# A two-image sparse attention kernel: new order ranks, a smaller ranking, products in pieces, and scatters and fetches of the first image that wait for the landing two places ahead

## The chip, the cores and the metric

The kernel runs on one core of a Trainium2 chip. Its time is the device time of one execution in microseconds (us), taken as the median over several runs. The profile is one execution of the same program, recorded by the hardware profiler; the times of instructions come from there. Engines are named as in the profile: PE is TensorE, PEld its weight load, DVE is VectorE, ACT is ScalarE, POOL is GpSimd, SP is SyncE, which only issues transfers here.

## The reference, cut to what matters

Two layers, each on images of 256 channels and 64 x 64 positions (N = 4096), two images. The first attends with sparsemax, the second with an unnormalised ReLU of a sum:

```python
# layer 0 (e: 64-channel conv 3x3 + batch norm + PReLU of x)
sim = einsum('bdn,bdm->bnm', e, e)
p   = sparsemax(sim, axis=2)          # threshold tau by the sorted row, max(sim - tau, 0)
x   = einsum('bcn,bnm->bcm', x, p) + x
# layer 1
g   = einsum('oc,bcn->bno', g_w, x) + g_b              # 128 channels
a   = w_t . theta(x);  bsc = w_p . phi(x)              # one number per position
f   = relu(a[:, :, None] + bsc[:, None, :] + wf_b)     # N x N
y   = matmul(f / N, g)
z   = batch_norm(wz @ y) + x
```

## The kernel before, in words

`sparse_path` computes everything; a dense path behind it stands for rows that the sparse one can't hold and is not run with this input.

**Layer 0.** After the convolution, `survey` (tiles sv) finds for each position whether its sparsemax row is the trivial one (only itself). `listed` gathers the few other rows into three blocks of 128. `rows` computes their similarities (PE, tile rw, L476; copy to z, L774; running maxima on DVE, L777), bisects the threshold and applies it. `attend` multiplies the kept columns: on POOL a product of x with a mask (L831, one per two 512-column blocks and channel half, with a small tick copy L826 ahead), on PE the product av (L836), on DVE the addition into x (L843). One matrix multiplication of the program is two MATMUL instructions in the trace.

**Layer 1.** f is a ReLU of a sum of two numbers, so y needs no N x N matrix: if positions are sorted by bsc, then the y of a position is made of two prefix sums over the sorted g. `project` (image 0, g, L873) and `project_in` (image 1, g, L899) compute g with the two extra columns (tile ga). The class `Ranked` then does, for its R row tiles of 128 positions (image 0: R = 32, all; image 1: R = 24, and the last 8 tiles are done densely: f on ACT L1512, py on PE L1520, `rest`):

- `keys` (L1000 on): sortable keys, made distinct from each other's neighbours by their low bits. `spread` turns them to rows on PE, writes them to memory (row_k to rd_k, L932) and reads them back to all partitions as kb (L944), both issued from SP.
- `above` for each row tile t: a pass over the columns of kb from tile t on that counts how many keys are larger, on ACT (Sign with accumulation, L1050) or DVE (is_gt with accumulation, L1054). Two slots or four of the junk ring take the results. `below` sums the same results over partitions on PE (L1065, L1076) for the later tiles; `below_out` (L1087) and `below_turned` (bt, L1093) bring these sums back to a column.
- `ties` (L1101): a DVE operation over the 128x128 block of the own tile, that adds equal keys further down by the triangular matrix `low`.
- `place` (L1115 to L1120) adds it all to a rank; `scatter` (L1125/L1126) writes the g row of each position to its rank in the memory table sg, an indirect DMA that POOL issues, one per row tile, with a memset ahead.
- `load` (L1141 to L1144) reads the sorted table into tab, in parts of 16 tiles (TH = 16); `products` (L1152/L1153) multiplies the g part by its key column, one operation per part; `sums` (L1160) adds up along the tiles, one dependent addition per tile; `before` (po, L1164) and `raised` (L1167) add what the partitions ahead hold; `stored` (L1173) writes the table tb.
- `segments` (oh, L1187/1188), `places` (pk, L1196) and `counts` (L1205 to L1208) find for each position its place k in the table; `fetch` (L1213) is an indirect DMA from POOL that brings the 128 rows of one tile of positions to a slot of r (16 slots; image by image 32 fetches).
- `taken` (L1226 on) combines a fetched row, turns it on PE (yr, L1233, yT, L1238 or L1240), and `finish` multiplies by wz (pz, L960), adds into x (L964) and stores to out (L967).

**What sets the order.** The class `Plan` writes the instruction order of every engine ahead of time: a list scheduler over tasks with a cost per engine, a latency (`lat`), and a rank; where several tasks can begin at about the same moment the lowest rank goes first. The ranks are 21 constants in L281 (RW1 for the rows of image 1, A1 for its attention, R0 and R1 for the beginnings of the rankings, K0 and K1 for their passes, CH0 and CH1 for the chains of load, products, sums, store and fetch, P1 and P2 for the projection, SP1 for spreading a, PY and PF for the dense part, BE for below, and so on). Where a task may go to DVE or ACT, the planner chooses too. At run time each engine executes its own list in order, and waits at an instruction until what it needs is there. SP's list holds the issue of the ordinary transfers, POOL's the mask products, scatters and fetches.

Of the kernel before, what the change touches and what calls it, by code (L numbers as in the profile page):

```python
# [8 lines left out]
F32 = mybir.dt.float32  # L9
BF16 = mybir.dt.bfloat16  # L10
# [4 lines left out]
ALU = mybir.AluOpType  # L15
# [4 lines left out]
P = 128  # L20
# [19 lines left out]
CS = 2 * CI + 1  # L40
TH = 16
# [149 lines left out]
def sparse_path(ctx: ExitStack, tc, a, out, rows_i):  # L191
    nc = tc.nc
# [787 lines left out]
    class Ranked:  # L980
# [55 lines left out]
        def above(self, t, on_act, d):  # L1036

            slot = d["slot"] = self.slot(self.used)
            self.used += 1
            kb, cnt, n = self.kb, self.cnt, self.R * P
            d["on_act"] = on_act
            c = ds(t * P, n - t * P)
            if on_act:
                nc.scalar.activation(  # L1050
                    slot[:, c], kb[:, c], AF.Sign, scale=STEEP, bias=self.bound[:, 1, t : t + 1], accum_out=cnt[:, t, 3:4],
                )
            else:
                nc.vector.tensor_scalar(  # L1054
                    slot[:, c], kb[:, c], self.key[:, t : t + 1], None, ALU.is_gt, ALU.add, accum_out=cnt[:, t, 1:2],
                )
            if on_act:
                self.on_act.append(t)
# [36 lines left out]
                    start=True, stop=True,  # L1095
                )

        def ties(self, t):

            junk = small.tile([P, P], BF16, name=f"tied_{self.b}_{t}", tag="tied", bufs=1)  # L1100
            nc.vector.scalar_tensor_tensor(  # L1101
                junk, self.kb[:, ts(t, P)], self.key[:, t : t + 1], low,
                ALU.is_equal, ALU.mult, accum_out=self.cnt[:, t, 2:3],
            )

        def place(self, t0, bt):

            b, R = self.b, self.R
            for t in range(t0, t0 + 4):
                known = t * P - sum(u in self.on_act for u in range(t)) * (P // 2)
                known += (R - t) * P // 2 if t in self.on_act else 0
                nc.vector.memset(self.cnt[:, t, 0:1], float(known))  # L1115
            cnt = self.cnt[:, ds(t0, 4)]
            rk = small.tile([P, 4], F32, name=f"rk_{b}_{t0}", tag="rk", bufs=2)
            nc.vector.tensor_reduce(rk, cnt[:, :, 0:3], AX.X, ALU.add)  # L1118
            nc.vector.tensor_tensor(rk, rk, bt, ALU.add)
            nc.vector.scalar_tensor_tensor(self.rank[:, ds(t0, 4)], cnt[:, :, 3], 0.5, rk, ALU.mult, ALU.add)  # L1120

        def scatter(self, t):
            b = self.b
            gap = small.tile([1, 1], F32, name=f"gap_{b}_{t}", tag="gap")
            nc.gpsimd.memset(gap, 0.0)  # L1125
            rows = nc.gpsimd.indirect_dma_start(  # L1126
                out=self.sg,
                out_offset=bass.IndirectOffsetOnAxis(ap=self.rank[:, t : t + 1], axis=0),
                in_=self.ga[:, t, 0 : CI + 2],
                in_offset=None,  # L1130
            )
# [11 lines left out]
            nc.vector.memset(self.nxt, -3.0e38)  # L1143
            nc.sync.dma_start(out=self.nxt[0 : P - 1], in_=sv[1:P, 0, CI + 1 : CI + 2])  # L1144

        def products(self, h):
            b, R, tab = self.b, self.R, self.tab[h]
# [3 lines left out]
            t0, n = self.parts[h]  # L1151
            nc.vector.tensor_copy(self.kr[:, ds(t0, n)], tab[:, :, CI + 1])  # L1152
            nc.vector.tensor_mul(  # L1153
                tab[:, :, CI + 1 : CS], tab[:, :, 0:CI], tab[:, :, CI : CI + 1].to_broadcast([P, n, CI])
            )

        def sums(self, t0, t1):
            at = lambda t: self.tab[t // TH][:, t % TH]
# [51 lines left out]
        def fetch(self, t):  # L1210
            if t == 0:
                self.r = self.at("r", [P, TH, CS], F32)
            nc.gpsimd.indirect_dma_start(  # L1213
                out=self.r[:, t % TH],
                out_offset=None,
                in_=self.tb,
                in_offset=bass.IndirectOffsetOnAxis(ap=self.k[:, t : t + 1], axis=0),
            )
# [31 lines left out]
            finish(b, ds(i * CB, CB), scaled, "A" if rest is None else "D", rank, after, h)  # L1250

        def fetch_task(self, t, rank, after):
            self.fetched[t] = plan.task({"G": 1.27}, lambda: self.fetch(t), rank, after, lat=4.14)

        def begin(self, rank, after, ranked, chained, then, room):

# [3 lines left out]
            plan.task({"G": 0.2}, self.first, rank, [k], lat=2.3, take=hz, free=[hz])  # L1260
            sp = spread(f"k{self.b}", lambda: self.key, lambda: self.kb, 0, self.R, rank, [k])
            n = self.R * P
            self.places_done, self.ranked, places = [], [], []
            self.used = 0
            hb = ring_sim.hold()
            below, waiting, places = [], [], {}
            for t in range(self.R):
                r, m, d, q = ranked + t / 100.0, n - t * P, {}, t // 4
                hj, last = self.ring.hold(), t == self.R - 1
                u = plan.task(  # L1270
                    {"D": 0.25 + 0.00107 * m, "A": 0.66 + 0.00083 * m}, lambda e, t=t, d=d: self.above(t, e == "A", d), r,
                    [sp, *room], take=hj, free=[hj] if last else [],
                )
                self.ranked.append(u)
                tied = plan.task({"D": 0.36}, lambda t=t: self.ties(t), r + 0.02, [sp, *room])
                places.setdefault(q, []).extend([u, tied])
# [27 lines left out]

        def chain(self):
# [2 lines left out]
            ld = plan.task({"S": 0.1}, self.load, rk, self.places_done, lat=8.45)  # L1308
            t = ld
            for h in range(H):  # L1310
                t = plan.task({"D": 0.3 + 0.1375 * self.parts[h][1]}, lambda h=h: self.products(h), rk, [t])
# [60 lines left out]
    def constants():  # L1372
# [7 lines left out]
        for t, n, by_partition in ((iota, P, False), (lane, 1, True)):  # L1380
# [3 lines left out]
        nc.gpsimd.affine_select(  # L1384
            out=low, in_=onesq, pattern=[[-1, P]], compare_op=ALU.is_gt, fill=0.0, base=0, channel_multiplier=1
        )
        for k in range(8):
            nc.vector.memset(invk[:, k : k + 1], 1.0 / (k + 1))

# [116 lines left out]
    f = []  # L1506
# [445 lines left out]
```

## Time and profile before

| | |
|---|---|
| median of 14 runs | 710.24 us (703.04 to 713.14) |
| the profiled execution | 709.79 us, its span 708.1 us |
| mean granted TensorE clock | 0.904 |
| PE / DVE / ACT / POOL busy | 590.0 (83%) / 527.2 (74%) / 322.1 (45%) / 221.2 (31%) us |
| first rw of image 1 / first pass of ranking 0 | 373.95 / 392.0 us |
| first scatter / first load of image 0's table | 437.9 / 489.06 us |
| kb of image 1 issued / first use | 506.05 / 513.79 us |
| image 0's table raised / first fetch | 577.1 / 588.31 us |
| last fetch issued / end of span | 684.13 / 708.1 us |

The times in the last five rows are from the start of the span. A busy share is an average over stages: a stage is read from the time window in which it runs, and from the chain, which goes back from the last instruction to whatever released each step. "DMA to landing" is the time from the issue of a transfer to its completion.

### The profile page before, as it was taken

To read this page: it belongs to the slowest core of one execution; us is meant where nothing else is said; L and a number is where in the kernel's file an instruction comes from. 1 tells how busy PE (TensorE), PEld (TensorE's weight loads), DVE (VectorE), ACT (ScalarE), POOL (GpSimd) and SP (SyncE) were. 2 spreads that over 40 slices of the span, in tenths; PEclk is the share of its full clock that TensorE was granted. 3 is DMA by queue.
4 is the path that set the end of the run, shared out by engine and by line. 5 is a ranking of instruction groups with operands and counts; after the bars stand their busy time and mean duration, and the time that the engine had idled before them with its cause. 6 is when DMAs were issued, how large, how long until landed. Compare 5 with 4: busy or idle time off the path is not lost.

```text
span 708.1 us, 8398 instructions
## 1 busy us (share of the span) xinstructions
PE 590.0 (83%) x2835; PEld 282.1 (40%) x2835; DVE 527.2 (74%) x1074; ACT 322.1 (45%) x484; POOL 221.2 (31%) x290
## 2 busy tenths in 40 slices
PE   5998999999779799999987787999399994376762
PEld 4664444444332233343543223358244541254320
DVE  6985777877878978788758999833599852897761
ACT  0123576576439556467108985400398870000000
POOL 0117930000030130202030323684000776636750
PEclk9999999999879899999999798889699996667995
DMA  8621001101120000000023000014720166356861
GB/s 347 226 60 31 1 1 31 31 1 31 31 81 7 0 1 0 1 1 0 2 80 139 20 1 11 27 50 120 227 93 16 38 263 186 89 222 206 271 215 65
DMA packets 34268, 57.07 MB, mean 81 GB/s; under 512 B 12942, under 2 KB 21000, under 8 KB 33192
## 3 DMA queue, kind: packets, MB, share of 16 engines
q1 hardware_dynamic: 28440, 42.72, 18.1%
q0 software_dynamic: 5344, 13.14, 6.6%
q10 hardware_dynamic: 432, 0.59, 0.3%
q8 instruction: 24, 0.39, 0.2%
q14 instruction: 28, 0.23, 0.1%
HBM read 32.67 MB, written 21.66 MB: 77 GB/s over the span
## 4 chain that ended last, share of the span: by engine, by line
PE 54%; DVE 31%; DMA 6%; issue 5%; ACT 2%; POOL 0%; SPq 0%; DVEq 0%; ACTq 0%; POOLq 0%
PE sv L476 15%; PE av L836 10%; PE cv_in L363 6%; PE cv_out L363 6%; PE pz L960 4%; DVE junk L1054 4%; DVE mq L777 4%; DVE tied L1101 3%; DVE tab L1160 3%; DVE x L964 2%; PE g L873 2%; DVE tab L1167 2%; DVE xbs L524 2%; PE sv L508 2%; PE py L1520 2%
## 5 line engine op out<-in xcount | busy, mean ns | idle before, releaser
L528 ACT ACTIVATE sv<-sv,nthr 128x1024 f32<-128x1024 f32 (+1 forms) x133 | 131.2, 986 | 99.4 <-PE sv L508 47.9
L524 DVE TENSOR_TENSOR xbs<-sv,xbs 128x1024 f32<-128x1024 f32 (+1 forms) x120 | 130.7, 1089 | 37.4 <-PE sv L476 30.4
L476 PE MATMUL sv<-e 64*128 64x512 f32 x512 | 136.4, 643 | 5.8 <-ACT sv L528 4.4
L836 PE MATMUL av<-z,xbs 128*128 128x512 f32 x192 | 108.8, 690 | 4.9 <-DVE z L799 2.8
L1126 POOL DMA_INDIRECT sg<-ga,rank x56 | 55.6, 993 | 72.6 <-DVE rk L1118 51.6
L1213 POOL DMA_INDIRECT r<-tb,k x64 | 64.3, 1005 | 38.2 <-issue 14.3
L1050 ACT ACTIVATE junk<-kb,bound 128x2816 bf16<-128x2816 f32 (+26 forms) x39 | 69.9, 1799 | 10.8 <-PE below L1076 7.8
L476 PEld LDWEIGHTS sv<-e 64*128 64x128 f32 x512 | 45.7, 195 | 72.1 <-issue 42.7
L1520 PE MATMUL py<-f,ga 128*128 128x512 f32 x128 | 64.2, 642 | 0.0
L836 PEld LDWEIGHTS av<-z,xbs 128*128 128x128 f32 x192 | 36.6, 213 | 62.0 <-issue 49.0
L363 PE MATMUL cv_out<-v,wu 128*64 128x256 f32 (+1 forms) x384 | 49.2, 395 | 7.7 <-DVE v L325 7.7
L446 POOL TENSOR_TENSOR sq<-es 128x512 f32<-128x512 f32 x8 | 9.6, 1198 | 133.6 <-ACT es L437 111.2
L1238 ACT ACTIVATE yT<-yr 128x512 f32<-128x512 f32 x8 | 4.8, 597 | 95.8 <-PE yr L1233 89.0
L1233 PE MATMUL yr<-ident,r 128*128 128x128 f32 x64 | 16.8, 344 | 37.4 <-DVE r L1226 37.3
L363 PE MATMUL cv_in<-v,wu 128*64 128x256 f32 (+1 forms) x384 | 46.6, 383 | 1.0 <-ACT c L374 1.0
L1054 DVE TENSOR_SCALAR_CACHE_REDUCE junk<-kb,ga 128x2688 bf16<-128x2688 f32 (+13 forms) x17 | 40.5, 2381 | 4.0 <-DMA kb<-rd_k 4.0
L843 DVE SCALAR_TENSOR_TENSOR x<-av,b,x 128x512 f32<-128x512 f32 x32 | 23.7, 747 | 24.8 <-PE av L836 23.6
L960 PE MATMUL pz<-yT,wz_sb 128*128 128x512 f32 x64 | 37.6, 714 | 4.4 <-DVE yT L1240 2.7
L363 PEld LDWEIGHTS cv_out<-v,wu 128*64 128x64 f32 x384 | 28.5, 141 | 31.6 <-issue 14.2
L1512 ACT ACTIVATE f<-ab,ga 128x1024 f32<-128x1024 f32 x32 | 35.7, 1141 | 8.0 <-PE py L1520 7.9
L363 PEld LDWEIGHTS cv_in<-v,wu 128*64 128x64 f32 x384 | 27.9, 137 | 21.5 <-issue 10.0
L1226 DVE SCALAR_TENSOR_TENSOR r<-r,a 128x128 f32<-128x128 f32 x64 | 19.6, 346 | 22.5 <-DMA r<-tb,k 22.3
(217 smaller groups left out, 858.3 us busy)
## 6 DMA issues: line engine op xcount, KB each, us to landing
out<-x SPq DMA_DIRECT2D x32, 256.0 KB, 3.6
tb<-tab SPq DMA_DIRECT2D x3, 2056.0 KB, 7.8
x<-in_x SPq DMA_DIRECT2D x8, 512.0 KB, 8.8
tab<-sg SPq DMA_DIRECT2D x3, 1040.0 KB
x<-in_x SPq DMA_DIRECT2D x4, 544.0 KB, 7.7
e<-e SPq DMA_DIRECT2D x16, 128.0 KB, 2.4
et<-es SPq DMA_DIRECT2D x16, 128.0 KB, 2.1
mask<-kd SPq DMA_DIRECT2D x2, 1024.0 KB, 4.7
```

The lines of the kernel that those rows point to most:

```text
L363: nc.tensor.matmul(d[jp, g][ts(h, CR), n, (r0 - r) * HH : (r1 - r) * HH], lhsT=taps(j, kc, dy), rhs=v[:, kc, r0 + dy - 1 : r1 + dy - 1], s ...
L476: nc.tensor.matmul(ps[:, ts(h, CB)], lhsT=lhs(h), rhs=e[ts(h, CR), q], start=True, stop=True)
L524: nc.vector.tensor_tensor(out=acc[:, cols], in0=d[i, q][:, cols], in1=acc[:, cols], op=ALU.max)
L528: nc.scalar.activation(ps, ps, AF.Relu, bias=both["nthr"][:, i : i + 1], accum_out=got_s["over"][:, i, q : q + 1])
L836: nc.tensor.matmul(pss[j, ct], lhsT=got["xb"][:, k, ts(ct, P)], rhs=got["zs"][k][:, ts(j, CB)], start=(k == 0), stop=(k == KB - 1),)
L960: nc.tensor.matmul(d["z"][:, ct], lhsT=wz_sb[:, ts(ct, P)], rhs=d["y"], start=True, stop=True)
L1050: nc.scalar.activation(slot[:, c], kb[:, c], AF.Sign, scale=STEEP, bias=self.bound[:, 1, t : t + 1], accum_out=cnt[:, t, 3:4],)
L1054: nc.vector.tensor_scalar(slot[:, c], kb[:, c], self.key[:, t : t + 1], None, ALU.is_gt, ALU.add, accum_out=cnt[:, t, 1:2],)
L1126: rows = nc.gpsimd.indirect_dma_start(out=self.sg, out_offset=bass.IndirectOffsetOnAxis(ap=self.rank[:, t : t + 1], axis=0), in_=self.ga[: ...
L1213: nc.gpsimd.indirect_dma_start(out=self.r[:, t % TH], out_offset=None, in_=self.tb, in_offset=bass.IndirectOffsetOnAxis(ap=self.k[:, t : t ...
L1512: nc.scalar.activation(fm, am, AF.Relu, bias=bm)
L1520: nc.tensor.matmul(pys[q][:, ts(h, CB)], lhsT=ga1[0][:, m, 0:CI], rhs=f[0][:, m % 4, ts(h, CB)], start=(m == NR), stop=(m == NT - 1),)
```

## The change

Five things at once:

1. The 21 rank constants of L281 are other numbers, so the planner writes another order from the first convolution on.
2. `above` begins one tile further right (at tile t+1 and not at t), and the pass for the last tile, which would be empty, goes: 54 passes for the two images, and not 56. The own tile is left to one DVE operation, `own`, of the same shape as `ties`: key difference compared with a triangle of tiny negative numbers, so that it counts larger keys and equal ones further down together. `low` is scaled once for it.
3. `products` is split: `keys_of` copies the key column of a part, and each four tiles are a piece of their own that goes to DVE (one multiplication) or ACT (four). The `sums` of two tiles wait for their piece only. In the order written, image 0 has four pieces on each engine, image 1 four on DVE and two on ACT.
4. A scatter of image 0, from the third on, has a second memset ahead on POOL, which overwrites an element of the ranks that the scatter two places ahead (AHEAD = 2) reads: it waits for that scatter's landing.
5. A fetch of image 0, from the third on, has a tick copy ahead on POOL, which reads the slot of the fetch two places ahead: it waits for that fetch's landing. The planner's costs of both become 1.7.

```diff
+AHEAD = 2
+TAU = 2.0**-90
...
-    DB, CV1, LS, RW0, SV1, RW1, A0, G0, A1, R0, K0, CH0, R1, K1, CH1, P1, P2, SP1, PY, PF, BE = -15.47, 6.58, -12.34, -12.34, -12.37, -24.38, 6.88, -11.7, -0.72, -32.06, -0.3, 11.42, 11.12, 11.73, 6.58, -24.23, -0.6, 10.82, 17.06, 12.47, -12.07
+    DB, CV1, LS, RW0, SV1, RW1, A0, G0, A1, R0, K0, CH0, R1, K1, CH1, P1, P2, SP1, PY, PF, BE = -13.93, 6.58, -13.63, -13.63, -13.75, -16.77, -8.26, -8.17, -0.75, -1.27, 14.19, -1.07, 5.2, -1.28, 6.84, -14.56, -11.28, 6.54, 2.8, 7.28, -1.94
...
         def above(self, t, on_act, d):
-            c = ds(t * P, n - t * P)
+            c = ds(t * P + P, n - t * P - P)
...
-        def ties(self, t):
+        def own(self, t):
             nc.vector.scalar_tensor_tensor(
                 junk, self.kb[:, ts(t, P)], self.key[:, t : t + 1], low,
-                ALU.is_equal, ALU.mult, accum_out=self.cnt[:, t, 2:3],
+                ALU.subtract, ALU.is_gt, accum_out=self.cnt[:, t, 2:3],
             )
...
         def scatter(self, t):
             b = self.b
+            self.sent.append(t)
             gap = small.tile([1, 1], F32, name=f"gap_{b}_{t}", tag="gap")
             nc.gpsimd.memset(gap, 0.0)
+            if self.b == 0 and len(self.sent) > AHEAD:
+                nc.gpsimd.memset(self.rank[0:1, ds(self.sent[-1 - AHEAD], 1)], 0)
             rows = nc.gpsimd.indirect_dma_start(
...
-        def products(self, h):
+        def keys_of(self, h):
...
+            nc.vector.tensor_copy(self.kr[:, ds(t0, n)], self.tab[h][:, :, CI + 1])
+
+        def products(self, e, i):
+            tab = self.tab[4 * i // TH][:, ds(4 * i % TH, 4)]
+            if e == "A":
+                for t in range(4):
+                    nc.scalar.mul(tab[:, t, CI + 1 : CS], tab[:, t, 0:CI], tab[:, t, CI : CI + 1])
+            else:
+                nc.vector.tensor_mul(
+                    tab[:, :, CI + 1 : CS], tab[:, :, 0:CI], tab[:, :, CI : CI + 1].to_broadcast([P, 4, CI])
+                )
...
         def fetch(self, t):
             if t == 0:
                 self.r = self.at("r", [P, TH, CS], F32)
+            if self.b == 0 and t >= AHEAD:
+                tick = small.tile([1, 1], F32, name=f"fetched_{self.b}_{t}", tag="gap")
+                nc.gpsimd.tensor_copy(tick, self.r[0:1, (t - AHEAD) % TH, 0:1])
             nc.gpsimd.indirect_dma_start(
...
-            self.fetched[t] = plan.task({"G": 1.27}, lambda: self.fetch(t), rank, after, lat=4.14)
+            self.fetched[t] = plan.task({"G": 1.27 if self.b else 1.7}, lambda: self.fetch(t), rank, after, lat=4.14)
...
-                            self.places_done.append(plan.task({"G": 1.28}, lambda i=i: self.scatter(i), ranked, [pl], lat=2.3))
+                            self.places_done.append(plan.task({"G": 1.28 if self.b else 1.7}, lambda i=i: self.scatter(i), ranked, [pl], lat=2.3))
...
+            made = [
+                plan.task({"D": 0.75, "A": 1.36}, lambda e, i=i: self.products(e, i), rk + i / 100.0, [lims]) for i in range(R // 4)
+            ]
             for i in range(R // 2):
-                t = plan.task({"D": 0.87}, lambda i=i: self.sums(2 * i, 2 * i + 2), rk + 0.5, [t])
+                t = plan.task({"D": 0.87}, lambda i=i: self.sums(2 * i, 2 * i + 2), rk + 0.5, [t, made[i // 2]])
```

How the written order moves (positions in the lists, which are the same in every run): before, the last mask products of image 1 and its products av lie among the passes of ranking 0 and behind them, the load of image 0's table precedes image 1's keys on SP, and the last four fetches of image 0 follow those of image 1 on POOL. After, the g of the last tiles of image 0 and one av move behind the start of image 1's rows, the keys of image 0 follow those rows, four mask products stay beside ranking 0 and all precede the first scatter, the whole av and most of the g of image 1 precede its keys, kb of image 1 precedes the load of image 0's table on SP, the sums and raising of image 0 are spread among the passes of ranking 1, and all fetches of image 0 precede those of image 1.

More of the change, by code (lines that the diff above doesn't have):

```diff
@@ L1096, in below_turned @@
                 )
-        def ties(self, t):
-            junk = small.tile([P, P], BF16, name=f"tied_{self.b}_{t}", tag="tied", bufs=1)
+        def own(self, t):
+            junk = small.tile([P, P], BF16, name=f"own_{self.b}_{t}", tag="tied", bufs=1)
             nc.vector.scalar_tensor_tensor(
                 junk, self.kb[:, ts(t, P)], self.key[:, t : t + 1], low,
-                ALU.is_equal, ALU.mult, accum_out=self.cnt[:, t, 2:3],
+                ALU.subtract, ALU.is_gt, accum_out=self.cnt[:, t, 2:3],
             )
@@ L1113, in place @@
                 known = t * P - sum(u in self.on_act for u in range(t)) * (P // 2)
-                known += (R - t) * P // 2 if t in self.on_act else 0
+                known += (R - 1 - t) * P // 2 if t in self.on_act else 0
                 nc.vector.memset(self.cnt[:, t, 0:1], float(known))
@@ L1144, in load @@
             nc.sync.dma_start(out=self.nxt[0 : P - 1], in_=sv[1:P, 0, CI + 1 : CI + 2])
-        def products(self, h):
-            b, R, tab = self.b, self.R, self.tab[h]
+        def keys_of(self, h):
+            b, R = self.b, self.R
+            t0, n = self.parts[h]
             if h == 0:
@@ L1150, in products @@
                 nc.vector.tensor_scalar_mul(self.kr[:, R : R + 1], lane, float(R))
[L1151 to L1155, printed above, removed]
+            nc.vector.tensor_copy(self.kr[:, ds(t0, n)], self.tab[h][:, :, CI + 1])
[8 more added lines that the diff above has]
+                )
         def sums(self, t0, t1):
@@ L1262, in begin @@
             n = self.R * P
+            self.sent = []
             self.places_done, self.ranked, places = [], [], []
@@ L1267, in begin @@
             for t in range(self.R):
-                r, m, d, q = ranked + t / 100.0, n - t * P, {}, t // 4
+                r, m, d, q = ranked + t / 100.0, n - t * P - P, {}, t // 4
                 hj, last = self.ring.hold(), t == self.R - 1
[L1270 to L1276, printed above, removed]
+                tied = plan.task({"D": 0.36}, lambda t=t: self.own(t), r + 0.02, [sp, *room])
+                places.setdefault(q, []).append(tied)
+                if not last:
+                    u = plan.task(
+                        {"D": 0.25 + 0.00107 * m, "A": 0.66 + 0.00083 * m}, lambda e, t=t, d=d: self.above(t, e == "A", d), r,
+                        [sp, *room], take=hj,
+                    )
+                    places[q].append(u)
+                    self.ranked.append(u)
                 if not last:
@@ L1310, in chain @@
             for h in range(H):
-                t = plan.task({"D": 0.3 + 0.1375 * self.parts[h][1]}, lambda h=h: self.products(h), rk, [t])
+                t = plan.task({"D": 0.25}, lambda h=h: self.keys_of(h), rk, [t])
             lims = plan.task({"D": 0.25}, self.limits, rk, [t])
+            made = [
+                plan.task({"D": 0.75, "A": 1.36}, lambda e, i=i: self.products(e, i), rk + i / 100.0, [lims]) for i in range(R // 4)
+            ]
             for i in range(R // 2):
-                t = plan.task({"D": 0.87}, lambda i=i: self.sums(2 * i, 2 * i + 2), rk + 0.5, [t])
+                t = plan.task({"D": 0.87}, lambda i=i: self.sums(2 * i, 2 * i + 2), rk + 0.5, [t, made[i // 2]])
             h0 = ring_av.hold()
@@ L1386, in constants @@
         )
+        nc.vector.tensor_scalar_mul(low, low, -TAU)
         for k in range(8):
```

## The prediction

> **What bounds the kernel now.** I read the page's busy shares first, then the chain of waits in order of time, then busy time by stage in windows, and last the engine timelines and the tiles sg (scattered rows) and r (fetched rows). TensorE is busy for 83% of the span and VectorE for 74%, but in different places. The windows show it: columns are busy us (and instructions) of PE, weight loads, DVE, ACT, POOL, then granted clock, DMA share, GB/s.
>
> ```profile
> 392.00:437.00 45.00, 35.56 (x157) 12.14 (x155) 44.37 (x73) 35.52 (x27) 13.73 (x13) 0.90 0.00 1
> 437.00:465.00 28.00, 24.41 (x113) 12.01 (x113) 21.00 (x96) 13.93 (x25) 19.44 (x33) 0.83 0.10 32
> 465.00:494.00 29.00, 29.00 (x158) 20.43 (x157) 9.25 (x22) 0.51 (x2) 18.83 (x35) 0.93 0.27 80
> 494.00:514.00 20.00, 7.51 (x29) 5.08 (x27) 10.16 (x17) 5.55 (x10) 0.34 (x2) 0.66 0.73 228
> 514.00:545.00 31.00, 29.14 (x151) 13.81 (x151) 30.19 (x69) 28.35 (x27) 0.00 (x0) 1.00 0.20 60
> 545.00:577.00 32.00, 32.00 (x123) 15.22 (x122) 29.65 (x94) 24.81 (x35) 21.70 (x39) 1.00 0.22 83
> 588.00:640.00 52.00, 26.64 (x88) 15.67 (x88) 39.61 (x78) 2.81 (x4) 29.89 (x29) 0.64 0.56 177
> 640.00:685.00 45.00, 33.63 (x105) 17.04 (x105) 32.89 (x78) 2.39 (x4) 34.34 (x36) 0.89 0.76 237
> ```
>
> The ranking of image 0 (392 to 465) is DVE's. From 465 to 494 PE alone is full, at 494 to 514 nobody is, then DVE and PE both, and after 588 POOL's fetches set the pace. The chain names the joints (start, length, what):
>
> ```profile
> 464.39 15.51 PE av L836 x30
> 479.90 8.07 PE g L899 x72
> 488.08 2.71 PE g L899 x24
> ...
> 503.22 2.82 DMA rd_k<-row_k
> 506.05 7.71 DMA kb<-rd_k
> 513.79 3.29 DVE junk L1054 x2
> ...
> 568.42 8.69 DVE tab L1167 x2
> 577.14 10.29 DMA tb<-tab
> ```
>
> The hole at 494 to 514 is the keys of image 1, written out and spread back as kb, behind the load of image 0's table on SP's queue. The last two views are the landings of the scatters (first line, tile sg) and fetches (second, tile r), and POOL's stalls among the fetches:
>
> ```profile
> DMA to landing us min/median/max: 2.3/2.3/9.0
> DMA to landing us min/median/max: 2.8/3.6/6.8
> ```
> ```profile
> 615.73 1.08 POOL L1213 DMA_INDIRECT r<-tb,k  x1 [0.30 <-issue]
> 623.43 1.07 POOL L1213 DMA_INDIRECT r<-tb,k  x1 [6.63 <-PE yr L1233]
> 632.10 0.95 POOL L1213 DMA_INDIRECT r<-tb,k  x1 [5.07 <-PE yr L1233]
> ```
>
> Undisturbed fetches follow each other at 1.26 us; the first 32 take 588.31 to 644.62, 1.8 each, as 16 slots must be emptied.
>
> **The small edits.** A pass over one block less: a DVE pass of 3712 columns takes 4.075 us and one of 2688 takes 3.008, so 0.133 us per 128; ACT 0.11 (3.746 for 4096, 3.637 for 3968). With 54 passes shorter and two of 0.4 gone that is some 7 us over both engines, and in ranking 0, where new ranks give DVE ten passes (22,400 columns) and not nine (19,968), nothing is left of it: 24.2 us against 22.7. The test of the own tile has the same operands and size (0.35 + 0.08). Products in pieces: 2.29 per 16 tiles becomes 0.57 per four; half go to ACT in image 0, so DVE saves 2.2 us, and ACT's 16 multiplications of 128x128 (at most 0.4 each, its smallest pass, 6.4 in all) lie in a stretch where it is 28 of 31 busy, but the sums of 0.43 a tile (1.7 per piece) need a piece only every 1.7 us. No row shows these multiplications; at nothing to 0.2 us each I take nothing, for DVE's chain of 30 sums covers them, and 3 us if it doesn't.
>
> **The waits on landings.** A scatter of image 0 now waits until the one two places ahead has landed: with landing 2.3 (its median and minimum), memset 0.09 and 0.3 to the issue, two go in 2.7, 1.35 each against 1.27 now. Thirty-two lose 3 us, or at landing 9.0 much more. Behind them on POOL's queue stand the scatters of image 1, and on SP's the load of image 0's table; DVE meanwhile has 29 us of passes and own-tile tests of image 1. So nothing, and 3 us without that cover. In the new order all mask products of image 1 (2.13 each) precede the scatters on POOL, so no attention work is queued behind a wait.
>
> The fetch is dearer. It waits for the landing two ahead, so two are in flight: landing 2.8, a tick of 0.2 (like POOL's tick copies), 0.25 to the issue: 3.25 for two, c = 1.63 each. Behind the wait on POOL stand only later fetches, image 1's last of all, and DVE waits for the rows. With the median landing, 3.6, c = 2.03; with 6.8, 3.6. I take 2.8, since 3.6 was measured with about three in flight and 237 GB/s beside them. [...]
>
> **The new order.** All 21 rank constants change, and with them almost every position after the first convolution. What matters, in order:
>
> 1. To the first row block of image 1 (PE rw, now 373.95). 32 g of 0.129 and 6 av of 0.5, 7.1 us of PE, move behind it, but they covered gathers of 2.7 us landing: between -7.1 and +2.7, middle -2.2: 371.8. The rows stage then takes its 25.9 (DVE threshold work) to 397.7.
> 2. The keys of image 0 now come after that stage and not inside it. kb lands some 15 us later (1.8 keys, 0.6, then 3.4 and 9.9 for the two transfers, as at 378.6 to 392.0): 413.4. DVE stands idle there; PE covers with av of image 1.
> 3. From 397.7 to the last g that image 1's keys need, PE has all 96 av (4 in 1.98, 48.0), 27.5 for the count sums (60.0 busy between 392 and 465, less 65 av of 0.5), and 96 g (8.07 per 72, 10.8): 86.3. Now the same stretch loses 13% (60.0 and 25.8 busy in the 98.8 from 392.0 to 490.8); the later full stretches lose 0 to 6%. I take 5%: 90.8, to 488.5. DVE's part of ranking 0 is smaller: 24.2 passes, 12.6 own tiles, 8.6 x additions, 2.1 + 6.5 for ranks, 4 ga, 5 lost: 63 from 413.4, to 476. Keys come 2.7 after the last g: 491.2.
> 4. Spread of these keys: on SP kb now stands ahead of the table load, so it costs its own 0.6 + 2.8 + 7.7: 502.3, where now it is 513.8. This is the change's one large gain, 11.5 us.
> 5. DVE from there to the raising of image 0's table: passes 19.2 (16,896 columns, eleven passes), own tiles 9.4, count rows and ranks 7.0, products 2.7, sums 14.3, one-hot rows 9.3, counts 3.9, raising 8.9, rest 1.3: 76.0. Now some 10 us of these (products, one-hot, sums) fill the hole at 494. At 95% (59.8 of 63 now) 80.0: 582.3. PE has some 80 from 488.5 (108 py at 0.45, 48.6; the last g 3.6; count sums and turns of ranking 1 about 20; places 8) and is done at 569, covered. So 5.2 us later than 577.1: the hole's gain is spent on work that used to lie in it.
> 6. Table store and first fetch as now, 11.2: 593.5. Thirty-two fetches at 1.63: 645.7. Then all of image 1, 31 x 1.26: last one at 684.8, where now it is 684.13. The last four of image 0 no longer come behind those of image 1, and the time from the last fetch to the use of its row, now 7.2 us, falls to a landing of 3.6: 24.0 after the last fetch becomes 20.4. Span 705.2.
>
> The mask products cost DVE now: six own-tile tests took 1.7 to 2.26 us instead of 0.35, each beside one of them.
>
> ```profile
> 407.36 2.13 POOL L831 TENSOR_TENSOR x<-x,mask 128x1024 f32<-128x1024 f32 x1
> ```
> ```profile
> 407.40 2.24 DVE L1101 SCALAR_TENSOR_TENSOR tied<-kb,ga,low 128x128 bf16<-128x128 f32 x1
> ```
>
> Eight lay in ranking 0, four still do, hence the 5 lost. [...]
>
> **The sum.** Span 705.2 and 1.7 around it (709.79 less 708.1) make 706.9; the median lies 0.45 above the profiled run: 707.3, told as 707. What a measurement can tell from no change is 0.3%, 2.1 us: below 708.1 is faster, above 712.4 slower.
>
> **Rivals.** (B) Slower: the fetch wait takes the end. From c = 1.79, a landing of 3.1 us, the time is above 712; at 2.03 the sum is 720, at 3.6 it is 770. For it: the median 3.6, and landings of 6.2 for the first fetches. Against it: those had a table load beside them, and the fetches now average 1.8 anyway. 0.24. (C) No gain or slower: the idle DVE at 398 to 413 isn't made up, PE loses 13% from then on as now, 99.2 for 86.3, and all behind comes 8.4 later than with 5%: 716, or 711 if half of it. For it: today's loss in that same stretch. 0.18. (D) Faster: c = 1.4 as DMA is quieter (-7.4), PE without loss (-4.5), rows stage 7.1 earlier: 688 with all of it, mostly 690 to 700. 0.20. Forecast, 700 to 711: 0.38.
>
> **How the numbers follow.** Faster: 0.27 of the forecast and all of D, 0.47. Same: 0.11 of the forecast, 0.04 of C, 0.15. Slower: B and 0.14 of C, 0.38. The range 690 to 724 leaves out c above 2.2 and everything of D that adds up, about 0.15. The forecast's own range is 700 to 711.
>
> **What would show it.** Right: kb of image 0 landing near 413 with DVE idle before it, image 1's kb near 502, table store near 582, fetches of image 0 at 1.6 each without long stalls on PE yr, the last fetch near 685. Wrong: scatters or fetches at 2 us or more, a hole still before image 1's ranking, or a convolution and survey stage that ends more than 7 us away from 374.

## Result: slower, 730.3 us, and the profile after

The changed kernel takes 730.34 us (median of 10 runs, 728.45 to 733.32), the kernel before 710.42 (median of 47): a ratio of 1.0293, interval 1.0268 to 1.0318. The forecast was 707, with a range of 690 to 724. Its profiled execution has a span of 727.1 us.

Up to the first fetch there is no loss, although almost every instruction has moved: it is issued at 588.50, and before at 588.31. The 19 us all lie behind it. Windows of the profile after, cut at the last fetch of image 0 and the last of image 1 (busy us of PE, weight loads, DVE, ACT, POOL; granted clock; DMA share; GB/s):

```profile
588.00:657.00 69.00, 44.71 (x100) 22.61 (x100) 41.56 (x87) 4.18 (x7) 39.38 (x62) 0.56 0.46 151
657.00:697.00 40.00, 26.19 (x50) 10.33 (x50) 19.00 (x43) 0.60 (x1) 30.47 (x32) 0.74 0.63 183
697.00:727.00 30.00, 13.15 (x24) 5.06 (x23) 9.13 (x21) 0.00 (x0) 0.11 (x1) 0.70 0.23 79
```

Two things differ from the rows of before. The fetches take longer: all 64 are out at 696.16 and not at 684.13. And the granted clock stands at 0.56, 0.74 and 0.70, where before it was 0.64 in the stage of image 0's fetches, 0.89 in that of image 1's, and 0.56 behind the last fetch:

```profile
685.00:708.00 23.00, 8.59 (x15) 2.96 (x15) 5.38 (x13) 0.60 (x1) 0.09 (x1) 0.56 0.23 81
```

The time behind the last fetch grew from 24.0 to 30.9 us. POOL's timeline in a quiet stretch of image 0 and at the worst place (start, length, what, idle ahead and who ended it):

```profile
604.06 0.98 POOL L1229 DMA_INDIRECT r<-tb,k  x1 [0.49 <-issue]
605.05 0.18 POOL L1228 COPY fetched<-r 1x1 f32<-1x1 f32 x1
605.53 0.98 POOL L1229 DMA_INDIRECT r<-tb,k  x1 [0.31 <-issue]
607.05 0.18 POOL L1228 COPY fetched<-r 1x1 f32<-1x1 f32 x1 [0.54 <-DMA r<-tb,k]
607.72 0.98 POOL L1229 DMA_INDIRECT r<-tb,k  x1 [0.48 <-issue]
...
641.11 0.98 POOL L1229 DMA_INDIRECT r<-tb,k  x1 [0.40 <-issue]
648.58 0.18 POOL L1228 COPY fetched<-r 1x1 f32<-1x1 f32 x1 [6.49 <-DMA r<-tb,k]
649.24 0.98 POOL L1229 DMA_INDIRECT r<-tb,k  x1 [0.48 <-PE yr L1249]
```

The copy that waits for the fetch of 604.06 begins at 607.05, 2.99 us later, and the next fetch but one goes out at 607.72: 3.66 us for two. At 641 the same wait lasts 6.49 us, while the store of image 1's table (2056 and 1028 KB) fills the DMA engines (last columns: clock, share of DMA, GB/s):

```profile
640.00:650.00 10.00, 5.88 (x11) 2.42 (x11) 5.95 (x11) 0.60 (x1) 2.50 (x5) 0.63 0.98 388
```

Now the chain of waits in image 1, one group of four rows (pieces under 0.3 us are left out, here and in the next view):

```profile
673.50 0.70 DVE yT L1256
674.25 3.37 PE pz L962 x4
677.64 0.75 DVE x L966
678.65 0.66 DVE x L966
679.63 0.35 PE yr L1249
680.00 0.70 DVE yT L1256
680.74 3.05 PE pz L962 x4
```

and in the kernel before:

```profile
664.82 0.61 DVE yT L1240
665.48 2.00 PE pz L960 x4
667.50 0.75 DVE x L964
668.51 0.66 DVE x L964
669.43 0.66 DVE x L964
670.10 0.61 DVE yT L1240
670.75 2.00 PE pz L960 x4
```

The same four matmuls take 2.0 us there and, in seven of the eight groups, 3.0 to 3.7 here, in a loop in which each engine waits for the next: 5.3 us a group then, 6.2 to 6.8 behind each of the slow ones now, for four fetches that at 1.26 us each need only 5.0. The granted clock differs with it. It is 0.50 where four pz take 3.78 us (from 660.55, changed kernel) and 1.00 where they take 1.98 (from 670.75, kernel before):

```profile
660.00:664.00 4.00, 3.45 (x4) 1.41 (x5) 0.70 (x2) 0.49 (x1) 3.09 (x4) 0.50 0.62 184
```
```profile
668.00:672.00 4.00, 2.78 (x11) 1.30 (x10) 3.31 (x8) 0.60 (x1) 3.08 (x4) 1.00 0.88 293
```

Half clock below means the first of the two. The order has thinned out PE's work there: before, groups of image 0 still lie among those of image 1 (105 matmul instructions, 33.63 us busy, in the 45 us from 640), now image 1's stand alone (50, 26.19 us, in the 40 us from 657). So O and K below don't exclude each other.

### The profile page after: what moved, and what is told of

It reads as the page before. It is cut to its first block, busy times and chain, and to the rows that moved or that the text cites. A ratio compares the mean times of both kernels' runs of the same rounds, so it can differ in the third digit from the quotient of the medians.

```text
span 727.1 us, 8554 instructions
## 1 busy us (share of the span) xinstructions
PE 611.2 (84%) x2835; PEld 294.1 (40%) x2835; DVE 526.9 (72%) x1085; ACT 320.8 (44%) x498; POOL 228.4 (31%) x350
## 4 chain that ended last, share of the span: by engine, by line
PE 56%; DVE 25%; DMA 8%; issue 6%; POOL 2%; ACT 2%; SPq 0%; DVEq 0%; POOLq 0%; ACTq 0%
PE sv L478 15%; PE av L838 10%; PE pz L962 7%; PE cv_out L365 6%; PE cv_in L365 6%; DVE junk L1056 3%; DVE mq L779 3%; DMA sg<-ga,rank 2%; DVE x L966 2%; DVE own L1104 2%; DVE xbs L526 2%; DMA r<-tb,k 2%; PE g L875 2%; PE pk L1209 2%; POOL sg L1132 1%
## 5 line engine op out<-in xcount | busy, mean ns | idle before, releaser
L478 PE MATMUL sv<-e 64*128 64x512 f32 x512 | 138.0, 649 | 6.2 <-ACT sv L530 5.2
L838 PE MATMUL av<-z,xbs 128*128 128x512 f32 x192 | 102.8, 661 | 9.1 <-DVE ga L881 9.1
L1052 ACT ACTIVATE junk<-kb,bound 128x2816 bf16<-128x2816 f32 (+23 forms) x33 | 59.1, 1791 | 25.2 <-DMA kb<-rd_k 11.2
L962 PE MATMUL pz<-yT,wz_sb 128*128 128x512 f32 x64 | 56.5, 1036 | 11.9 <-DVE yT L1256 6.4
L1543 PE MATMUL py<-f,ga 128*128 128x512 f32 x128 | 62.1, 632 | 4.3 <-ACT f L1535 4.3
L1056 DVE TENSOR_SCALAR_CACHE_REDUCE junk<-kb,ga 128x2944 bf16<-128x2944 f32 (+16 forms) x21 | 45.3, 2157 | 18.4 <-DMA kb<-rd_k 15.3
L966 DVE SCALAR_TENSOR_TENSOR x<-pz,s,x 128x512 f32<-128x512 f32 x32 | 23.2, 747 | 38.7 <-PE pz L962 38.7
L1249 PE MATMUL yr<-ident,r 128*128 128x128 f32 x64 | 21.5, 384 | 29.8 <-DVE r L1242 28.0
L1543 PEld LDWEIGHTS py<-f,ga 128*128 128x128 f32 x128 | 24.4, 199 | 31.7 <-issue 26.7
```

The source lines that it names most:

```text
L478: nc.tensor.matmul(ps[:, ts(h, CB)], lhsT=lhs(h), rhs=e[ts(h, CR), q], start=True, stop=True)
L838: nc.tensor.matmul(pss[j, ct], lhsT=got["xb"][:, k, ts(ct, P)], rhs=got["zs"][k][:, ts(j, CB)], start=(k == 0), stop=(k == KB - 1),)
L962: nc.tensor.matmul(d["z"][:, ct], lhsT=wz_sb[:, ts(ct, P)], rhs=d["y"], start=True, stop=True)
L966: nc.vector.scalar_tensor_tensor(xc, d["z"][:, ct], s1[:, ct : ct + 1], xc, ALU.mult, ALU.add)
L1052: nc.scalar.activation(slot[:, c], kb[:, c], AF.Sign, scale=STEEP, bias=self.bound[:, 1, t : t + 1], accum_out=cnt[:, t, 3:4],)
L1056: nc.vector.tensor_scalar(slot[:, c], kb[:, c], self.key[:, t : t + 1], None, ALU.is_gt, ALU.add, accum_out=cnt[:, t, 1:2],)
```

## Experiments

Theories: W, the waits on landings are the loss; O, the new order is; K, TensorE's half clock in the stage of the fetches is. Each ratio is against the kernel before on the same chip.

### The waits taken out

All waits (the order of the other instructions stays as written):

```diff
-AHEAD = 2
+AHEAD = 99
```

> The changed kernel with its order kept (same ranks, same planner costs) and neither the scatters' memset nor the fetches' tick ahead: nothing waits for a landing two places back. Theory W (the fetch waits are the loss): fetches of image 0 again 1.26 us apart until the 16 slots are full, first fetch still near 588, time 708 to 714. Theory O (the loss is the new order, in which image 1's fetches all come last, and its sums lie among image 0's fetched rows): 725 to 731, as with the waits. Theory K (the loss is the half clock of TensorE in this phase, whatever paces it): above 720, with pz still at 3.8 us for four.

722.61 us, ratio 1.0201 (1.0139 to 1.0264). Neither W nor O: 0.9% comes back, 2.0% stay. The fetches of image 0 go out mostly 1.26 us apart, the last at 627.51, 28 us earlier than with waits, and POOL then stands idle until image 1's table is stored:

```profile
627.51 0.95 POOL L1229 DMA_INDIRECT r<-tb,k  x1 [0.30 <-issue]
648.20 0.95 POOL L1229 DMA_INDIRECT r<-tb,k  x1 [19.74 <-DMA tb<-tab]
```

So image 1's first fetch waits here for its own table, and not for image 0's fetches. What follows in the chain is the loop again, with four pz at 3.65 to 3.69 us as at half clock, and a period that hardly moves (pz begins at 673.51, 680.28, 687.08, 693.89, 700.71, 707.52):

```profile
679.53 0.70 DVE yT L1256
680.24 0.04 issue
680.28 3.67 PE pz L962 x4
683.98 0.75 DVE x L966
684.73 0.26 DVE r L1242
684.99 0.66 DVE x L966
685.65 0.27 DVE r L1242
685.92 0.04 issue
685.97 0.34 PE yr L1249
686.33 0.70 DVE yT L1256
687.03 0.04 issue
687.08 3.69 PE pz L962 x4
```

The last fetch is out at 687.42, and 34.9 us follow it. So K is alive, and the waits are a smaller part than W says.

One kind at a time. Fetch ticks out:

```diff
-            if self.b == 0 and t >= AHEAD:
+            if self.b == 0 and t >= 99:
```

> The changed kernel without the tick ahead of the fetches alone, scatter waits kept. Theory W: like the kernel without any of the waits within 2 us, 708 to 714, since the scatters' waits lie beside image 1's keys and passes. If the scatter waits cost something, some 3 to 6 us more than without any.

725.27 us, 1.0235 (1.0182 to 1.0289). Scatter memsets out:

```diff
-            if self.b == 0 and len(self.sent) > AHEAD:
+            if self.b == 0 and len(self.sent) > 99:
```

> The changed kernel without the memset that waits for a scatter, fetch waits kept. Theory W: 727 to 731, no gain, though the last scatter of image 0 is issued some 10 us earlier than at 504. Rival (scatters hold up the first table load and so everything behind): 718 to 724.

727.93 us, 1.0274 (1.0218 to 1.033). The first load of the table is issued at 497.3 and not at 506.4, and the first fetch at 587.5 and not at 588.5: the scatters' waits are covered, as the prediction had it. The difference between no waits and no fetch waits, 2.7 us, lies within the intervals.

The tick on the slot four places back:

```diff
-            if self.b == 0 and t >= AHEAD:
+            if self.b == 0 and t >= 4:
...
-                nc.gpsimd.tensor_copy(tick, self.r[0:1, (t - AHEAD) % TH, 0:1])
+                nc.gpsimd.tensor_copy(tick, self.r[0:1, (t - 4) % TH, 0:1])
```

> The changed kernel with the fetch's tick reading the slot of the fetch four places ahead and not two; scatter waits kept. Four in flight at a landing of 3.0 allow 0.9 us a fetch, so the wait should hardly bite: fetches at 1.4 to 1.5 us (1.26 and the tick), last fetch of image 0 near 636 instead of 656, time 722 to 727 like the version without fetch waits. If the tick itself and not the landing is the price: 728 to 731.

726.30 us, 1.0234 (1.0179 to 1.0288), like the version without fetch waits. The time is as expected, but image 0's last fetch goes out at 649 and not near 636 (the slots and the store hold it), and the loop of image 1 runs at half clock here too (3.50 to 3.68 for four pz, 6.7 to 6.8 apart). With the clock low, how fetches are paced shows little: 0.6% between this run and the change as written.

The tick alone in the order of before:

```diff
+AHEAD = 2
...
             if t == 0:
                 self.r = self.at("r", [P, TH, CS], F32)
+            if self.b == 0 and t >= AHEAD:
+                tick = small.tile([1, 1], F32, name=f"fetched_{self.b}_{t}", tag="gap")
+                nc.gpsimd.tensor_copy(tick, self.r[0:1, (t - AHEAD) % TH, 0:1])
```

> The kernel before, with nothing but the tick ahead of each fetch of image 0 from the third on (the planner's cost unchanged, so the order is that of before): what the wait costs where the rest is as it was. Theory W: fetches at 1.9 us instead of 1.26 with stalls (1.8 on the mean), so +2 to +6 in the first 28, then 712 to 718. If the waits also cost the clock in the old order: 718 to 726.

721.08 us, 1.0218 (1.0134 to 1.0302), 11 us above the median of before, 15 by the ratio, and more than W expected. The median of its pz stays at 0.59 us (half clock: 1.06), and the last fetch goes out at 693.06 instead of 684.13. The granted clock is 0.86 in the stage of image 1's fetches, against 0.89 before. So this is in the main the price of the fetch waits where TensorE mostly has its clock.

### TensorE kept busy

The products of the identity with itself, five in each of the 16 groups, go to places that the real ones overwrite; DVE, POOL, SP and the order are not touched:

```diff
             def turned(t):
...
+                for _ in range(3 if t % 4 == 2 else 0):
+                    nc.tensor.transpose(d["ps"][:, t % 4], ident, ident)
                 nc.tensor.transpose(d["ps"][:, t % 4], self.r[:, t % TH, 0:CI], ident)
...
+            for _ in range(0 if ct else 2):
+                nc.tensor.matmul(d["z"][:, 0, 0:P], lhsT=ident, rhs=ident, start=True, stop=True)
             nc.tensor.matmul(d["z"][:, ct], lhsT=wz_sb[:, ts(ct, P)], rhs=d["y"], start=True, stop=True)
```

Without waits:

> The changed kernel without waits, and with TensorE kept busier where fetched rows are taken: three more transposes of the identity ahead of every third yr of four, overwritten by the real one, and two more 128x128 products of the identity ahead of pz, overwritten too (32 x 5 small matmuls in 16 groups; DVE, POOL and the order are untouched). Theory K (the tail is long since TensorE is granted half its clock, four pz take 3.7 us instead of 2.0, eight groups of image 1 in a row): granted clock near 1.0 from 590 on, four pz in 2.0, a group of image 1 in 5.1 us instead of 6.8, time 703 to 711 against 722.6. Theory O (the order alone: image 1 behind image 0, whatever the clock): 721 to 728, since the added matmuls only fill waits or lengthen them.

705.93 us, 0.9945 (0.9903 to 0.9987): 16.7 us less by adding work, and faster than the kernel before. PE's timeline in image 1:

```profile
676.53 1.98 PE L964 MATMUL pz<-yT,wz_sb 128*128 128x512 f32 x4 [0.34 <-DVE yT L1260]
678.35 0.38 PE L1253 MATMUL yr<-ident,r 128*128 128x128 f32 x2
678.57 0.49 PE L1252 MATMUL yr<-ident 128*128 128x128 f32 x3
679.62 0.33 PE L1253 MATMUL yr<-ident,r 128*128 128x128 f32 x1 [0.56 <-DVE r L1244]
680.54 0.33 PE L1253 MATMUL yr<-ident,r 128*128 128x128 f32 x1 [0.59 <-DVE r L1244]
680.71 0.61 PE L963 MATMUL pz<-ident 128*128 128x128 f32 x4
681.66 1.98 PE L964 MATMUL pz<-yT,wz_sb 128*128 128x512 f32 x4 [0.34 <-DVE yT L1260]
```

Every one of image 1's pz groups takes 1.98 now, 5.12 us apart. The windows of its fetches, first without and then with the added matmuls, show what changed: 3 us more PE work in 40 us, and the granted clock from 0.76 to 0.96.

```profile
648.00:688.00 40.00, 26.09 (x48) 10.61 (x47) 18.49 (x42) 0.60 (x1) 30.34 (x32) 0.76 0.61 174
```
```profile
644.00:684.00 40.00, 29.30 (x114) 15.75 (x114) 21.92 (x50) 0.60 (x1) 30.48 (x32) 0.96 0.65 190
```

K holds. With waits the same filling is too weak:

> The changed kernel with both kinds of wait, and the same added matmuls in the taking of fetched rows. Theory K: four pz in 2.0 us here too; the fetches of image 0 still set their pace of 1.9 us and the two stalls beside the store of the second table (8 and 4 us), so 714 to 720. If waits and clock are the same loss (the waits only matter through the clock): 703 to 711. Theory O: 727 to 733.

726.19 us, 1.0224 (1.0076 to 1.0373), the widest spread of all, and above what K expected. In its profile a gap of PE between two rows reaches 3.02 us (at 654.86) while fetches stall; three groups of image 1 in a row, from 673.74 to 690.8, run pz in 3.5 to 3.6 us and a later one in 3.33, the other four in 1.98. So the filling was doubled:

```diff
-                for _ in range(3 if t % 4 == 2 else 0):
+                for _ in range((0, 0, 6, 3)[t % 4]):
...
-            for _ in range(0 if ct else 2):
+            for _ in range(0 if ct else 4):
```

> The changed kernel with both kinds of wait and about twice the added matmuls (6 and 3 ahead of the third and fourth yr, 4 ahead of pz). In the weaker version four of the eight groups of image 1 still ran at half clock. Theory K: clock at 1.0 in image 1, its groups in 5.1 us, so the last use of a fetched row follows the last fetch by some 4 us and the time is 714 to 719; what is left over 706 is the price of the waits themselves. If waits alone explain the loss and the clock does not: 724 to 730.

718.04 us, 1.0121 (1.0072 to 1.0171), as K expects, with image 1's pz at 1.98 throughout. All fetches and the last group:

```profile
L1231 POOL DMA_INDIRECT r<-tb,k x64: 950/977/1339, 587.9 to 696.4; - x64
703.80 1.98 PE L964 MATMUL pz<-yT,wz_sb 128*128 128x512 f32 x4
```

The last fetch is where it was as written (696.4 against 696.16), but 20.1 us follow it (span 716.5) and not 30.9: the clock made the tail long, and here it did not delay the fetches. And without waits:

> The changed kernel without waits, with the stronger filling. Theory K: three of image 0's groups that still ran at half clock (629 to 647) speed up, the second table is raised up to 4 us earlier: 701 to 705. If the added matmuls now stand in the way of the real ones (more than fits into the waits): 706 to 712.

706.76 us, 0.9958 (0.9931 to 0.9986): no further gain over the weaker filling, where K expected 701 to 705. The median pz is 0.59 us, and in 15 of the 16 groups DVE waits for it, 29.5 us in all, 1.97 a group: the clock is there in image 0 too now, but image 1's first fetch still goes out at 645.52 (644.07 with the weaker filling). The last fetch is issued at 684.9, 11.5 us before that of the run with waits: that is where the waits cost.

> The kernel before with the weaker filling and nothing else. Theory K: it has the full clock for image 1 anyway (four pz in 2.0), so there is little to win: the last group's pz (2.9 to 3.8 us) and three of image 0's, 703 to 710. Rival (filling helps whatever the clock, by some other way): as much as in the changed kernel without waits, 17 us, 692 to 696.

710.79 us, 1.0018 (0.9991 to 1.0044). Where four pz mostly take 2.0 us anyhow the added matmuls bring nothing, which excludes the rival's 17 us: what they bring in the changed kernel comes with the clock.

These make a table (ratio to the kernel before; the last column is from one chip):

| | as written | filled (stronger) |
|---|---|---|
| both waits | 1.0293 | 1.0121 |
| no waits | 1.0201 | 0.9958 |

The clock, by what the filling gives back, costs 1.7% with waits and 2.4% without, 12 and 17 us. The waits cost 0.9% as written and 1.6% with the filling, 7 and 12 us. Each of these is good to some 0.6%, by the intervals of its two ratios. Whether the half clock hides part of the waits is not shown: the difference, 0.7%, is no larger than the noise of four such ratios.

### Ranks and small edits

The changed kernel with the old ranks (L281 as before):

> The changed kernel with the 21 rank constants of before: pieces, own tile and both kinds of wait stay, the planner writes the order anew. Theory W: the waits cost as much in the old order, 722 to 735, fetches of image 0 at 1.9 us. Theory O: the loss goes with the new order, 705 to 713.

724.04 us, 1.0249 (1.0183 to 1.0314): the waits come with their price in a third order too. The first 23 fetches of image 0 take 595.48 to 644.90, 2.25 each with two stalls of over 5 us, and its last nine follow those of image 1; the scatters' waits are not covered in this order, the first table load moves from 489.06 to 499.3, and the first fetch 7 us with it (that the waits do this is argued, not separated). The median pz is 0.59 us: with both waits in place and the old ranks TensorE mostly keeps its clock, so it is the new order, and not the waits, that goes with the half clock.

The kernel before with the new ranks alone:

> The kernel before with nothing but the 21 new rank constants (56 passes, ties, products whole, no waits). Theory K and O alike: the new order costs what the kernel without waits shows, 718 to 728, with pz at half clock. If the pieces and the own tile are what the new ranks were for: even slower, above 728. If the order alone is harmless: 706 to 713.

755.53 us, 1.0671 (1.0585 to 1.0756). The planner writes another order again: here image 1's kb stands behind the load of image 0's table on SP and is issued at 505.2, and the first fetch goes out at 614.62. The ranks belong to the costs and tasks they were chosen with; this run prices neither alone.

The small edits alone (old ranks, planner costs 1.27 and 1.28, no waits), and the filled kernel without waits with these costs:

```diff
-            self.fetched[t] = plan.task({"G": 1.27 if self.b else 1.7}, lambda: self.fetch(t), rank, after, lat=4.14)
+            self.fetched[t] = plan.task({"G": 1.27}, lambda: self.fetch(t), rank, after, lat=4.14)
```

> The kernel before with the small edits alone: shorter passes (54), own tile, products in pieces; old ranks, planner costs 1.27 and 1.28, no waits. The prediction put these edits at nothing. If so: 707 to 712. Rival: their 7 us of shorter passes and 4.6 us of split products do come through: 698 to 705. Or they upset the old order, for which the ranks were not made: 713 to 725.

> The changed kernel without waits and with the weaker filling, and with the planner told 1.27 and 1.28 for fetches and scatters of image 0, which is what they then cost: a candidate for the fastest. If the written order is better with true costs: 698 to 704; if the costs matter little: 704 to 708, like the version with 1.7.

790.28 and 795.32 us, 1.0663 and 1.0693, on a chip on which the kernel before takes 741.53. Both again, beside the filled version with the planner's costs at 1.7, on that same chip:

> The small edits alone (shorter passes, own tile, products in pieces; old ranks, planner costs of before, no waits), on another chip: on the first one the kernel before itself took 741 us, so that run can't be read. In that run's trace seven scatters of image 1 stand behind all fetches of image 0 on POOL, so the second table is loaded only at 656. That is the written order and goes with the kernel: if it is the cost, 725 to 770 here too. If the chip was the cost: 705 to 715.

> The changed kernel without waits, weaker filling, planner costs 1.27 and 1.28, on another chip. In the first run its chain had 15% in stalls of ACT and PE that nothing in the trace releases. If these were the chip's: 698 to 712 here. If the order written with these costs is the loss: 730 or more, with image 1's kb behind the table load on SP (520 instead of 489).

> The changed kernel without waits and with the weaker filling, a second time for the comparison with the two beside it on one chip: 704 to 708 where the kernel before takes 710, a ratio of 0.992 to 0.998. On a chip like the first one of the last call it would be above 740.

795.79, 795.79 and 764.93 us against 743.24: 1.0706, 1.0691 and 1.0293. On this chip ACT (and through it the rest) stands still at places where the trace names no releaser in the program, up to 21 us at a time; in the filled version's chain such pieces hold 8.0% of the span. One of them on ACT's timeline:

```profile
462.81 0.19 ACT L1054 ACTIVATION_READ_ACCUMULATOR junk<-kb,bound 128x1 f32 x1
470.62 0.61 ACT L1054 ACTIVATE junk<-kb,bound 128x384 bf16<-128x384 f32 x1 [7.63 <-remote]
```

What the chip's stalls are stays open. So the filled kernel without waits beats the kernel before on two chips by 0.6% (weaker filling) and 0.4% (stronger), and loses 2.9% on this one. The planner's costs of 1.27 and 1.28 make it 31 us slower here, with no larger a share of such pieces (6% in the first of its two runs): in the order written with them image 1's kb is issued behind the load of image 0's table on SP (519.67 and 514.24 in that run), with 1.7 ahead of it (489.08 and 498.07 on the other chip; kb at 504.9 on this one). For the small edits one reading doesn't depend on the chip: in their written order the last seven scatters of image 1 stand behind all fetches of image 0 on POOL, and the load of image 1's table stands on SP behind stores to out (issued at 656, before at 588). How much that order costs on another chip wasn't measured.

## Why the prediction was wrong, step by step

**Right, within 8 us.** Steps 1 to 5. Image 1's rows begin at 363.78 (371.8 predicted; over 7 us from 374 was on its own list of signs of being wrong), kb of image 0 is first used at 407.7 (413.4 predicted), image 1's kb at 498.7 (502.3), DVE's work from there to the raising takes 81 us (80.0), the table is raised at 579.7 (582.3), the first fetch goes out at 588.5 (593.5). The hole at 494 to 514 did close, and its gain was spent on work that used to lie in it. The scatters were mis-sized (1.71 us each, 450.86 to 504.02, and not 1.35), but covered as said.

**The step that failed is 6.** Its terms:

| | predicted | measured |
|---|---|---|
| first fetch | 593.5 | 588.5 |
| from it to image 1's first fetch | 52.2 | 68.6 |
| image 1's fetches | 39.1 | 39.1 |
| after the last fetch | 20.4 | 30.9 |
| span | 705.2 | 727.1 |

The fetch term was c = 1.63 for "landing 2.8, a tick of 0.2, 0.25 to the issue". The landing was about right (median 3.0), but the way from tick to issue took 0.48 on the slower side, and the mean of the first 27 steps was 1.95; with two stalls of 8.1 and 3.9 us between fetches beside the store of image 1's table it is 2.17. The stalls are what the sum left out: it took the landing of a quiet DMA and didn't ask what else moves when image 1's table is stored. That table has no term of its own in the sum either: at c = 1.63 image 1's fetches simply follow image 0's, at 645.7. Without waits image 0's were out at 627.51, and image 1's first still went out only at 648.20, behind the store. So 645.7 lies near what the table allows by luck, and rival D's c of 1.4 would have gained little. No run shows 1.4: it would have needed a landing of about 2.3 us, and the least of a fetch is 2.8 in this trace and 2.7 without waits; the quickest two steps between fetches of image 0 took 3.55 us here, 1.78 each. Rival B had this mechanism, with 0.24, and by its own rule 2.17 would have given about 725.

The tail term took over the 24.0 us of before, less 3.6 for a row used sooner, and with them the pace of before's groups, most with four pz in 2.0 us. It never asked whether TensorE would still be granted its clock in the new order, though the prediction's own rows have it at 0.64 and 0.89 in the two stages of the fetches. No rival named it. With four pz at 1.98 us all through image 1 the tail comes out as predicted: 21.3 us without waits (704.6 less 683.28) and 20.1 with them, against 20.4. Of the two terms the fetches missed by more, 16.4 us against 10.5, of which the earlier first fetch gave 5.0 back; by the runs the clock is worth 12 to 17 us and the waits 7 to 12, by which of them is taken out first.

**Small edits at nothing.** Not confirmed and not refuted: the runs that should have priced them moved the order. A piece of the products took 0.69 us on DVE (0.57 predicted), a multiplication on ACT 0.39 (at most 0.4).

**A slip in the sums.** Rival D takes the rows stage as 7.1 us earlier, though the sum has already taken 2.2 of that: all of D makes 690 or 691, not 688.

## What to carry to other kernels

The stage in which PE, DVE and DMA hand four tiles round in a loop had two speeds here, 5.1 and 6.8 us a group, and the granted clock told which (0.96 and 0.76 in the 40 us of image 1's fetches); an order that makes the work of PE sparser (33.63 us busy of 45 before, 26.19 of 40 after) can go with the slow one without adding any work. So check the clock of a stage before a matmul's duration is carried over to a new order. Where a wait on a landing paces a queue, price it at the landing beside the largest transfer that can run then (the copy's wait was 6.49 us beside the store of a table, and 0.54 in a quiet stretch), and look for what else it will hold. Rank constants and planner costs are one set: an edit of either writes a new program, and parts of such a change can't be priced by undoing one.

## What the runs showed of the hardware

The loop with four pz in 3.6 to 3.7 us (no waits) held for eight groups in a row, 6.72 to 6.82 us apart, and the one with 1.98 (no waits, weaker filling) did so at 5.11 to 5.20 us. In the 40 us of image 1's fetches PE is busy for 65% and 73% of the time (26.09 and 29.30 us), and the granted clock is 0.76 and 0.96. In the first loop the clock goes up and down, row by row of 4 us (0.89 from 676 to 680, 0.57 from 680 to 684), though no gap of PE from 672 to 690 is longer than 0.89 us. Between these two runs the clock went with the busy share of PE. The filling shortened the longest gap too, from 0.89 to 0.59 us, so which of the two counts is not separated. Why the clock falls and comes back within a group, and why the period stays at 6.78 us on the mean, is not shown.
